# Layer 1 of a mixed network: the x weights of all nine taps made once per sample, and four engine queues in a planned order

## The chip, the cores and the metric

The kernel runs on one core of a Trainium2 chip, in one launch. Its time is the device time of that core in microseconds. It computes a network of four layers on eight images; the change touches the second one, layer 1, a deformable convolution.

## What is computed

Each image has 256 channels and 32x32 pixels. Layer 1, cut to what matters:

```python
def deform_conv(x, offset, w):     # x [B,64,32,32], offset [B,18,32,32]: (dy,dx) per tap of 3x3
    ...
    py = gy + ky + dy              # where each tap of each pixel looks
    px = gx + kx + dx
    ...
    sampled = corner(y0, x0, wy0 * wx0) + corner(y0, x0 + 1, wy0 * wx1) \
            + corner(y0 + 1, x0, wy1 * wx0) + corner(y0 + 1, x0 + 1, wy1 * wx1)
    return einsum('bckhw,ock->bohw', sampled, w)
xd = relu(group_norm(conv1x1(x, w1), g1, b1))     # 256 -> 64 channels
offset1 = conv3x3(xd, w_off)                      # 64 -> 18
out = deform_conv(xd, offset1, w_def) + xd
out = relu(group_norm(conv1x1(out, w3), g3, b3)) + x
```

A bilinear sample is a sum over all pixels of the image, each weighted by a hat function of its distance in y times one in x: the weight is -min(|d| - 1, 0) in each direction, and zero for all but four pixels. The kernel uses this form.

## The kernel before

`fast1` is layer 1. Its generators are cut into steps by `yield`, and the order in which the steps are written into the program is set by `by_time`: each stream has a start, a distance between its steps and a generator, and the stream that is due first goes next. One unit of that time is one tap; a sample takes nine. The compiler then schedules each engine's queue from that order and from what depends on what.

`before(b)` loads a sample's `x` (L1769), takes it to 64 channels (`c1`, L1774; the two halves of the image lie in partitions 0 to 63 and 64 to 127 of `xd`), normalizes it, and computes the 18 offsets (`off`, L1799). `pos` (L1808, L1809) holds for every tap the y and x positions of the 1024 pixels. `pos` is stored to DRAM as `shifts` (L1811, four stores).

`taps(b)` multiplies `xd` by each tap's 64x64 weights, 128 pixels at a time, into `z` (L1825, L1835); every second result is copied out of PSUM by VectorE, every other one by ScalarE (L1828, L1838).

`main` runs over 8 samples x 9 taps. For each tap the row of x positions and the row of y positions are read from `shifts` and spread over 128 partitions (`row`, L1885, 512 KB each, two ahead). A partition stands for one source pixel of a group of 128 (four image rows); eight groups are handled as columns. ScalarE makes the distances in x (`ax`, L1896) and in y (`ay`, L1902, and for the image rows beyond a group's own L1906 to L1912); VectorE subtracts 1 and cuts at 0 (L1914, L1915), and multiplies the two into `wt` (L1917, L1921). Two taps later `add` (L1866) lets TensorE accumulate `z` times `wt` into `acc`, which holds the sample's whole image in PSUM. The accumulation of a sample begins at L1850, with the skip connection.

`after(b)` takes the finished sum `s` (copied at L1873) back to 256 channels (`c3`, L1937, copied out at L1938), normalizes (`group_norm`, L1747 to L1764), adds `x`, loaded again as `xr` (L1932), and stores the result (L1944, L1945).

Layers overlap. `net.head()` runs the next layer's first steps, up to its `HOLD`, between the last steps of the layer before; for layer 1 these are its weights and `before(0)`. What lies behind `HOLD` needs SBUF and PSUM space that the layer before gives back. `in_order` ties the instructions of an engine to the order in which they were traced; before the change, layer 0 alone uses it.

Of the kernel before, what the change touches and what calls it, by code (L numbers as in the profile page):

```python
# [18 lines left out]
B = 8  # L19
# [878 lines left out]
class Fast:  # L898


    def __init__(self, ctx, tc, dram, out):
        self.tc, self.nc, self.dram, self.out = tc, tc.nc, dram, out
        nc = self.nc
        self.const = ctx.enter_context(tc.tile_pool(name="const", bufs=1))
        self.dpool = ctx.enter_context(tc.tile_pool(name="acts", bufs=1, space=bass.MemoryType.DRAM))
        self.ident = self.const.tile([P, P], F32, name="ident")
        make_identity(nc, self.ident)
        self.unit = self.const.tile([P, P], F32, name="unit")
        nc.gpsimd.memset(self.unit, 1.0)
        self.mean = self.const.tile([P, P], F32, name="mean")  # L910
        nc.gpsimd.memset(self.mean, 1.0 / C)
        self.mean64 = self.const.tile([P, 64], F32, name="mean64")
        nc.gpsimd.memset(self.mean64, 1.0 / C)
        self.eps5 = self.constant(1e-5, "eps5")
        self.eps6 = self.constant(1e-6, "eps6")
        self.sums2 = self.dpool.tile([2 * B, HF], F32, name="sums2")
        self.sums3 = self.dpool.tile([8 * B, N], F32, name="sums3")
        self.shifts = [self.dpool.tile([2, 9, N], F32, tag=f"shifts{b}", name=f"shifts{b}") for b in range(B)]
        self.sums = self.dpool.tile([8 * B, HF], F32, name="sums0")
        self.groups, self.following, self.lent = {}, None, {}  # L920
# [236 lines left out]
def fast0(net, io):  # L1157
# [8 lines left out]
    with ExitStack() as ctx, ExitStack() as att:  # L1166
# [528 lines left out]
        by_time(rest + [[T * B + 9, 0.3, gates(B - 1, BY_PRODUCTS)], [T * B + 4, 1, net.head()]])  # L1695
# [3 lines left out]
def fast1(net, io):  # L1699
    tc, nc = net.tc, net.nc  # L1700
    D = 64
    with ExitStack() as ctx:
# [29 lines left out]
        axs = [wp.tile([P, R], F32, tag=f"ax{i}", name=f"ax{i}") for i in range(2)]  # L1732
        ays = [wp.tile([P, R + HF], F32, tag=f"ay{i}", name=f"ay{i}") for i in range(2)]
        for a in axs + ays:
            nc.gpsimd.memset(a, 0.0)
        xds, zs, ss, own = ({} for _ in range(4))
        pools, stored = [psM], set()

        def group_norm(x, gsel, g, b):


            n, halves = x.shape[1], x.shape[2] // HF
            st = two.tile([P, n, halves, 6], F32, tag=f"gn_st{n}", name="gn_st")
            mv = two.tile([P, 2, n], F32, tag=f"gn_mv{n}", name="gn_mv")
            for k in range(n):
                for h in range(halves):
                    nc.vector.bn_stats(st[:, k, h, :], x[:, k, bass.ts(h, HF)])  # L1747
                nc.vector.bn_aggr(mv[:, :, k], st[:, k])
            yield
            pm = bank("gn_m")  # L1750
            nc.tensor.matmul(pm[:, :n], lhsT=gsel, rhs=mv[:, 0], start=True, stop=True)
            t = two.tile([P, 4, n], F32, tag=f"gn_t{n}", name="gn_t")
            mean, d, var, shift = (t[:, i] for i in range(4))
            nc.vector.tensor_copy(mean, pm[:, :n])
            nc.vector.tensor_tensor(d, mv[:, 0], mean, ALU.subtract)
            nc.vector.tensor_tensor(var, d, d, ALU.mult)
            nc.vector.tensor_tensor(var, var, mv[:, 1], ALU.add)
            yield
            pv = bank("gn_v")
            nc.tensor.matmul(pv[:, :n], lhsT=gsel, rhs=var, start=True, stop=True)  # L1760
            net.rsqrt(d, pv[:, :n], net.eps5)
            nc.vector.tensor_tensor(d, d, g, ALU.mult)
            nc.vector.tensor_tensor(shift, mean, d, ALU.mult)
            nc.vector.tensor_tensor(shift, b, shift, ALU.subtract)  # L1764
            yield d, shift

        def before(b):
            x = one.tile([P, KC, N], F32, tag="x", name="x")
# [3 lines left out]
            for k in range(KC):  # L1772
                for h in range(2):
# [3 lines left out]
                    )  # L1777
            xd = xds[b] = two.tile([P, HF], F32, tag="xd", name="xd")
            nc.scalar.copy(xd, ps)
            yield  # L1780
            for norm in group_norm(xd.unsqueeze(1), gsel1, col(G1), col(B1)):
                yield
            nc.scalar.activation(xd, xd, AF.Relu, scale=norm[0], bias=norm[1])
            xp = xpads[b % 2]
            nc.vector.tensor_copy(xp[:, 1:17, 1 : 1 + IMG], img(xd))
            nc.scalar.copy(xp[0:64, 17, 1 : 1 + IMG], xd[64:128, 0:IMG])
            nc.scalar.copy(xp[64:128, 0, 1 : 1 + IMG], xd[0:64, HF - IMG : HF])
            yield

            pos = two.tile([P, HF], F32, tag="pos", name="pos")  # L1790
            pss = [bank("off") for _ in range(2)]
            for t in range(5):
# [11 lines left out]
                if t % 2:  # L1804
                    yield
            for h in range(2):
# [3 lines left out]
                for xy in range(2):  # L1810
                    nc.sync.dma_start(  # L1811
                        out=net.shifts[b][xy, :, bass.ts(h, HF)], in_=pos[64 * h + 9 * xy : 64 * h + 9 * xy + 9]
                    )
            stored.add(b)
            yield

        def taps(b):
# [3 lines left out]
            for c in range(4):  # L1821
                for h, copy in enumerate((nc.vector.tensor_copy, nc.scalar.copy)):
# [5 lines left out]
                    copy(z[:, 4 * h + c, :8].rearrange("p t o -> p (t o)"), ps)  # L1828
                    yield

            for h, copy in enumerate((nc.vector.tensor_copy, nc.scalar.copy)):
# [6 lines left out]
                copy(z[:, 4 * h : 4 * h + 4, 8], ps[:, : 4 * D].rearrange("p (c o) -> p c o", o=D))  # L1838
                yield

        def main():

            wts, accs = {}, {}
# [11 lines left out]
            def add(b, t):  # L1855
# [15 lines left out]
                if t == 8:  # L1871
                    ss[b] = own["r"].tile([P, N], F32, tag="s", name="s")
                    nc.scalar.copy(ss[b], acc)  # L1873
# [5 lines left out]
            def load(i, xy):  # L1879

                if i < len(steps):
                    b, t = steps[i]
                    assert b in stored
                    rows[i, xy] = row = own["rows"].tile([P, N], F32, tag=f"row{xy}", name=f"row{xy}")
                    nc.sync.dma_start(out=row, in_=net.shifts[b][xy, t : t + 1, :].to_broadcast([P, N]))  # L1885

            for i in range(2):
                for xy in range(2):
                    load(i, xy)
            for i, (b, t) in enumerate(steps):  # L1890
                ky = t // 3 - 1

                ax, ay = axs[t % 2], ays[t % 2]
                mine = slice((1 + ky) * IMG, (1 + ky) * IMG + N)
                px = rows.pop((i, 0))
                nc.scalar.activation(ax[:, mine], px, AF.Abs, bias=col(NQX))  # L1896
                load(i + 2, 0)
                if i > 1:
                    add(*steps[i - 2])
                yield  # L1900
                py = rows.pop((i, 1))
                nc.scalar.activation(ay[:, mine], py, AF.Abs, bias=col(NQR))  # L1902
                far = ay[:, R:].rearrange("p (c n) -> p c n", c=8)
# [5 lines left out]
                else:  # L1909
# [3 lines left out]
                load(i + 2, 1)  # L1913
                nc.vector.tensor_scalar(ax, ax, -1.0, 0.0, ALU.add, ALU.min)  # L1914
                nc.vector.tensor_scalar(ay, ay, -1.0, 0.0, ALU.add, ALU.min)  # L1915
                wt = wts[b, t] = own["wt"].tile([P, 8, 6 * IMG], F32, tag="wt", name="wt")
                nc.vector.tensor_tensor(  # L1917
                    wt[:, :, : 4 * IMG], ay[:, :N].rearrange("p (c n) -> p c n", c=8),
                    ax[:, :N].rearrange("p (c n) -> p c n", c=8), ALU.mult,
                )  # L1920
                nc.vector.tensor_tensor(  # L1921
                    wt[:, :, 4 * IMG :], far, ax[:, 4 * IMG :].rearrange("p (c n) -> p c n", c=8)[:, :, :64], ALU.mult
                )
                yield
            for s in steps[-2:]:
                add(*s)
                yield

        def after(b):
            s = ss[b]  # L1930
            x = own["r"].tile([P, KC, N], F32, tag="xr", name="xr")
            nc.sync.dma_start(out=x, in_=io.src[b])  # L1932
            c3 = own["r"].tile([P, KC, N], F32, tag="c3", name="c3")
            for k in range(KC):
                for h in range(2):
                    ps = bank("c3")
                    nc.tensor.matmul(ps, lhsT=w3[:, bass.ts(k, P)], rhs=s[:, bass.ts(h, HF)], start=True, stop=True)  # L1937
                    nc.scalar.copy(c3[:, k, bass.ts(h, HF)], ps)  # L1938
                yield
            for norm in group_norm(c3, gsel3, vec[:, G3 : G3 + KC], vec[:, B3 : B3 + KC]):  # L1940
                yield
            for k in range(KC):
                nc.scalar.activation(c3[:, k], c3[:, k], AF.Relu, scale=norm[0][:, k : k + 1], bias=norm[1][:, k : k + 1])
                nc.vector.tensor_tensor(x[:, k, :], x[:, k, :], c3[:, k], ALU.add)  # L1944
            nc.sync.dma_start(out=io.dst[b], in_=x)  # L1945
# [7 lines left out]
        own["rows"] = io.pool(ctx, "f1p", 2)  # L1953
        pools.append(io.pool(ctx, "f1n", 2, PSUM))
# [4 lines left out]
        taps_of_all = main()  # L1959
        streams = [(0, 0.5, taps_of_all)]  # L1960
        for b in range(B):
            if b:
                streams.append((T * (b - 1) + 0.7, 0.6, before(b)))
            streams.append((T * b - 3.1 if b else -1, 0.32 if b else 0.05, taps(b)))
            streams.append((T * (b + 1) + 2.3, 0.6, after(b)))
        rest = by_time(streams, until=taps_of_all)
# [1510 lines left out]
```

## Time and profile before

| | |
|---|---|
| median of 14 runs | 3995.0 us (3986.57 to 4004.31) |
| the profiled execution | 3989.45 us, span 3987.6 us |
| busy, whole span | PE 92%, DVE 63%, ACT 57%, POOL 17% |
| granted clock of TensorE, whole span | 0.958 |
| layer 1's first and last accumulating matmul (L1866) start | 1260.2 and 1632.9 us |

PE is TensorE, DVE VectorE, ACT ScalarE, POOL GpSimd, SP SyncE, which issues most DMAs; PEld are PE's weight loads. A line of a group of instructions has the source line, engine, operation, what is written and read with its shape, the count, then busy microseconds, mean nanoseconds of one, and the engine's idle time just before, with what ended it. A line of the windows view has a stretch, its length, each engine's busy time in it (with the number of instructions), the granted clock, the mean busy share of the 16 DMA engines and GB/s. A line of the waits view says who waited for whom: total microseconds, times, longest. Matmuls are pipelined and their ends are modelled; many matmuls of the same tile run side by side in the array, so the mean of one is longer than its share of the time.

### The profile page before, as it was taken

To read this page: it belongs to the slowest core of one execution; us is meant where nothing else is said; L and a number is where in the kernel's file an instruction comes from. 1 tells how busy PE (TensorE), PEld (TensorE's weight loads), DVE (VectorE), ACT (ScalarE), POOL (GpSimd) and SP (SyncE) were. 2 spreads that over 40 slices of the span, in tenths; PEclk is the share of its full clock that TensorE was granted. 3 is DMA by queue.
4 is the path that set the end of the run, shared out by engine and by line. 5 is a ranking of instruction groups with operands and counts; after the bars stand their busy time and mean duration, and the time that the engine had idled before them with its cause. 6 is when DMAs were issued, how large, how long until landed. Compare 5 with 4: busy or idle time off the path is not lost. (4 is left out here: it accounts for less than half of the span.)

```text
span 3987.6 us, 70125 instructions
## 1 busy us (share of the span) xinstructions
PE 3678.5 (92%) x28022; PEld 1699.3 (43%) x28022; DVE 2516.0 (63%) x5026; ACT 2290.7 (57%) x3106; POOL 689.4 (17%) x850
## 2 busy tenths in 40 slices
PE   8999999999899887899999869989999999998997
PEld 3223333333234444444444436553333333327886
DVE  2489999999987988522322457732555656567355
ACT  4566666666545777434343455417677667774453
POOL 1101111101010000000000024330000240054653
PEclk9999999999998988899999979989999999999998
DMA  3314323323234877301000123332320130155676
GB/s 118 90 56 124 116 97 104 115 93 94 72 102 152 285 270 256 125 1 41 23 22 22 43 77 115 113 122 71 112 92 33 59 103 33 36 173 182 211 234 208
DMA packets 191506, 438.11 MB, mean 110 GB/s; under 512 B 22201, under 2 KB 117388, under 8 KB 178628
## 3 DMA queue, kind: packets, MB, share of 16 engines
q1 hardware_dynamic: 149188, 317.34, 24.4%
q0 software_dynamic: 38320, 111.08, 8.8%
q8 instruction: 224, 3.67, 0.4%
q10 hardware_dynamic: 3664, 5.11, 0.4%
q14 instruction: 110, 0.90, 0.1%
HBM read 280.20 MB, written 160.18 MB: 110 GB/s over the span
## 5 line engine op out<-in xcount | busy, mean ns | idle before, releaser
L2876 ACT ACTIVATE e<-s,five 128x1024 f32<-128x1024 f32 x512 | 542.3, 1111 | 216.1 <-PE s L2870 204.0
L1291 DVE SCALAR_TENSOR_TENSOR a<-hp,w_f_vec,a 128x961 f32<-128x961 f32 (+1 forms) x496 | 608.3, 1233 | 26.9 <-ACT a L1534 17.1
L2870 PE MATMUL s<-q,k 32*128 32x512 f32 x2048 | 312.7, 641 | 1.4 <-issue 0.9
L2850 PE MATMUL A<-e,v 128*32 128x512 f32 x2048 | 274.7, 608 | 17.0 <-DVE o L2855 15.2
L1465 ACT ACTIVATE e<-s 128x1024 f32<-128x1024 f32 x256 | 247.3, 1017 | 30.7 <-PE s L1459 27.3
L2558 DVE SCALAR_TENSOR_TENSOR junk<-mo_x,w_f_wr 128x256 f32<-128x256 f32 x512 | 250.1, 489 | 13.5
L1403 PE MATMUL A<-e,va 128*32 128x512 f32 x2048 | 249.3, 605 | 0.0
L1026 PE MATMUL pi<-xn,w_l_wpi 128*32 128x512 f32 x2048 | 238.0, 603 | 11.0 <-DVE xn L1281 8.9
L1420 DVE TENSOR_TENSOR sum<-sum,e 128x1024 f32<-128x1024 f32 x188 | 221.0, 1219 | 29.0 <-ACT e L1465 29.0
L1866 PE MATMUL acc<-wt,z 128*64 128x192 f32 (+4 forms) x1344 | 132.8, 338 | 51.7 <-DVE wt L1921 51.4
L1058 POOL DMA_INDIRECT res<-y,to x149 | 149.5, 1004 | 129.3 <-DVE y L3101 65.0
L3077 PE MATMUL h<-xk,w 128*128 128x128 f32 x1192 | 153.4, 282 | 20.1 <-DVE xk L3063 14.4
L2870 PEld LDWEIGHTS s<-q,k 32*128 32x128 f32 x2048 | 92.9, 183 | 169.5 <-issue 163.4
L3046 ACT COPY w<-w_l3f_w 128x512 f32 x149 | 91.6, 628 | 124.7 <-PE h L3077 84.8
L1459 PE MATMUL s<-q,k 32*128 32x512 f32 x1024 | 156.2, 647 | 6.7 <-ACT e L1465 6.7
L3077 PEld LDWEIGHTS h<-xk,w 128*128 128x128 f32 x1192 | 149.6, 197 | 26.6 <-DVE xk L3063 15.8
L1058 POOL DMA_INDIRECT so<-xl,rows x128 | 130.0, 1016 | 171.2 <-issue 126.8
L3097 PE MATMUL y<-w_l3f_w,hid 128*128 x596 | 146.6, 388 | 4.7 <-issue 2.7
L1866 PEld LDWEIGHTS acc<-wt,z 128*64 128x64 f32 x1344 | 99.0, 152 | 101.4 <-DVE wt L1921 72.8
L1026 PEld LDWEIGHTS pi<-xn,w_l_wpi 128*32 128x32 f32 x2048 | 67.4, 111 | 163.9 <-issue 133.6
L1531 ACT ACTIVATE hp<-pi,pib 128x512 f32<-128x512 f32 x128 | 85.9, 686 | 89.3 <-PE pi L1026 87.2
L2184 POOL TENSOR_TENSOR x<-x,yn 128x1024 f32<-128x1024 f32 x16 | 37.3, 2351 | 572.5 <-ACT yn L2183 324.3
(425 smaller groups left out, 6985.5 us busy)
## 6 DMA issues: line engine op xcount, KB each, us to landing
row<-shifts SPq DMA_DIRECT2D x144, 512.0 KB
x<-d SPq DMA_DIRECT2D x31, 1024.0 KB
xs<-so SPq DMA_DIRECT2D x73, 260.0 KB
so<-zero SPq DMA_DIRECT2D x5, 3380.0 KB
thrice<-vimg POOLq DMA_DIRECT2D x64, 256.0 KB
xl<-mox SPq DMA_DIRECT2D x64, 256.0 KB
yg<-res SPq DMA_DIRECT2D x32, 512.0 KB
gated<-st POOLq DMA_DIRECT2D x28, 512.0 KB
```

The costliest lines, as they stand in the source:

```text
L1026: self.nc.tensor.matmul(ps[32 * h : 32 * h + 32], lhsT=lhsT[:, 32 * h : 32 * h + 32], rhs=rhs, **flags)
L1058: made = self.nc.gpsimd.indirect_dma_start(**args)
L1291: nc.vector.scalar_tensor_tensor(to, fr, taps(t_), to, ALU.mult, ALU.add)
L1403: nc.tensor.matmul(state["A"][32 * h : 32 * h + 32, c, :], lhsT=vas[b][:, kt, c, 32 * h : 32 * h + 32], rhs=e[h // 2][:, h % 2, :], start= ...
L1420: nc.vector.tensor_tensor(half, half, e[j], ALU.add)
L1465: nc.scalar.activation(es[i][j], ss[j], AF.Exp, scale=SCALE)
L1866: nc.tensor.matmul(acc[o, a * IMG : e * IMG], lhsT=zs[b][:, c, t, :], rhs=wt[:, c, (a - lo) * IMG : (e - lo) * IMG], start=False, stop=(t ...
L2558: nc.vector.scalar_tensor_tensor(junk, xn[:, t, :], 1.0, self.wr[:, e, :], ALU.mult, ALU.mult, accum_out=pr[:, t, e : e + 1])
L2850: nc.tensor.matmul(A[32 * h : 32 * h + 32], lhsT=vs[b][:, kt, c * P + 32 * h : c * P + 32 * h + 32], rhs=e[:, h, :], start=first, stop=last,)
L2870: nc.tensor.matmul(ss[h // 2][:, h % 2], lhsT=ks[b][32 * h : 32 * h + 32, c, bass.ts(kt, P)], rhs=qs[b][32 * h : 32 * h + 32, c, bass.ts(h ...
L2876: anchor[:] = [nc.scalar.activation(e[:, 2 * j : 2 * j + 2], ss[j], AF.Square, scale=SCALE, bias=five)]
L3077: nc.tensor.matmul(ps[:, j, m], lhsT=ws[j][:, k, bass.ts(m, P)], rhs=xk[:, j, k], start=(k == 0), stop=(k == KC - 1),)
```

## The change

The hat function in x depends on the image column of the source pixel and not on its image row: 32 partitions hold all that the 128 of a group need, for every group. So the change makes the x weights of all nine taps of a sample at once, in `before`: TensorE spreads each tap's row of positions over 32 partitions by a matmul with one column of the identity, for four quarters of the image side by side; ScalarE takes the distance out of PSUM, VectorE cuts it, and four DMAs store it in DRAM as `hats` (nine taps, 32 columns, 1024 pixels). For each tap `main` then loads finished x weights, spread from 32 to 128 partitions by the DMA, straight into `ax`. The x positions are no longer stored.

Beside that:
- all of `z` leaves PSUM by ScalarE, and its small last part by VectorE;
- VectorE's min over `ay` leaves out columns that aren't read;
- there are three `ax` and three `ay`; `hx` shares the buffer of `x`; the `x` of sample 1 lies where `c3` will be, in a pool opened behind `HOLD`;
- the stores of y positions, `hats` and results are issued by GpSimd;
- steps are cut finer, and a table (`BEFORE`, `TAPS`, `AFTER`) gives each one its place in units of taps; from time 0 on, the queues of TensorE, VectorE, ScalarE and SyncE keep the order of the table;
- the half of `before(1)` with negative times and all of `taps(0)` are traced ahead of that; in layer 0, `head` steps follow each other at 0.4 instead of 1, as there are more of them.

```diff
 before(b), behind the offsets:
-                for xy in range(2):
-                    nc.sync.dma_start(
-                        out=net.shifts[b][xy, :, bass.ts(h, HF)], in_=pos[64 * h + 9 * xy : 64 * h + 9 * xy + 9]
-                    )
+                nc.gpsimd.dma_start(
+                    out=net.shifts[b][1, :, bass.ts(h, HF)], in_=pos[64 * h + 9 : 64 * h + 18]
+                )
+                yield
             stored.add(b)
+
+            for n in range(6):
+                if n < 5:
+                    ps = bank("hx")
+                    for i in range(2 if n < 4 else 1):
+                        for j in range(4):
+                            r = 64 * (j // 2) + 2 * n + i
+                            nc.tensor.matmul(
+                                ps[32 * j : 32 * j + 32, bass.ts(i, C)],
+                                lhsT=net.ident[:, r : r + 1].to_broadcast([P, 32]), rhs=pos[:, bass.ts(j % 2, C)],
+                                start=True, stop=True,
+                            )
+                if n == 1:
+                    hx = one.tile([P, 9 * C], F32, tag="x", name="hx").rearrange("p (t n) -> p t n", n=C)
+                if n:
+                    part = slice(2 * n - 2, min(9, 2 * n))
+                    nc.scalar.activation(
+                        hx[:, part], held[:, : C * (part.stop - part.start)].rearrange("p (t n) -> p t n", n=C),
+                        AF.Abs, bias=col(NQX),
+                    )
+                held = ps
+                yield
+            nc.vector.tensor_scalar(hx, hx, -1.0, 0.0, ALU.add, ALU.min)
+            for j in range(4):
+                nc.gpsimd.dma_start(
+                    out=net.hats[b][:, :, bass.ts(j, C)].rearrange("t q n -> q t n"), in_=hx[32 * j : 32 * j + 32]
+                )
             yield
 main:
-                px = rows.pop((i, 0))
-                nc.scalar.activation(ax[:, mine], px, AF.Abs, bias=col(NQX))
...
+            def load(i):
+                if i < len(steps):
+                    b, t = steps[i]
+                    assert b in stored
+                    nc.sync.dma_start(
+                        out=axs[i % 3][:, place(t)], in_=net.hats[b][t].unsqueeze(0).to_broadcast([P // IMG, IMG, N])
+                    )
...
+            def weights(i):
+                b, t = steps[i]
+                ax, ay, mine = axs[i % 3], ays[i % 3], place(t)
+                far = ay[:, mine.stop : mine.stop + HF]
+                used = ay[:, mine.start : mine.stop + (448, 480, 512)[t // 3]]
+                nc.vector.tensor_scalar(used, used, -1.0, 0.0, ALU.add, ALU.min)
...
+            for i, (b, t) in enumerate(steps):
+                load(i + 2)
+                if i + 1 < len(steps):
+                    distances(i + 1)
+                    fetch(i + 3)
+                yield
+                if i > 1:
+                    add(*steps[i - 2])
+                yield
+                weights(i)
                 yield
 the order:
-        taps_of_all = main()
-        streams = [(0, 0.5, taps_of_all)]
-        for b in range(B):
-            if b:
-                streams.append((T * (b - 1) + 0.7, 0.6, before(b)))
-            streams.append((T * b - 3.1 if b else -1, 0.32 if b else 0.05, taps(b)))
-            streams.append((T * (b + 1) + 2.3, 0.6, after(b)))
-        rest = by_time(streams, until=taps_of_all)
+        BEFORE = (
+            -9, -6.7, -6.2, -5.5, -4.4, -3.8, -2.8, -2.3, -1.6, -1, -0.5, 1.1, 1.4, 1.7, 2, 2.3, 3, 3.2,
+            3.9, 4.2, 4.5, 4.8, 5.1, 5.4, 5.9,
+        )
+        TAPS = [1.6 + 0.72 * n + 0.5 * i for n in range(10) for i in range(2)]
+        AFTER = (
+            1.9, 1.95, 5.6, 6, 6.1, 6.5, 6.6, 7, 7.1, 7.5, 7.6, 7.8, 8.4, 9.3, 9.8, 10.6, 11, 11.6, 12.2, 12.5, 12.8, 13.4, 13.5
+        )
...
+        planned(0, [n + h for n in range(T * B + 2) for h in (0, 0.3, 0.7)], main_steps)
+        for b in range(B):
+            if b:
+                planned(T * (b - 1), BEFORE, before(b))
+            planned(T * (b - 1), TAPS, taps(b))
+            planned(T * (b + 1), AFTER, after(b))
+        times.sort(key=lambda t_: t_[0])
...
+        run(0)
+        kinds = mybir.EngineType
+        with net.in_order(kinds.PE, kinds.DVE, kinds.Activation, kinds.SP):
+            run(T * B + 2)
```

`fetch(i)` loads the row of y positions of a tap as `load(i, 1)` did, `distances(i)` is ScalarE's part of the old loop for y, and `weights(i)` ends with the two products of the old loop.

## The prediction

> **What bounds the kernel now.** I read the page first: the span is 3987.6 us and PE is busy for 92% of it, so I looked for the stretch in which the changed function works, by asking for layer 1's accumulating matmul (L1866): 1260 to 1633 us. Then I cut that stretch into sample periods. ACT copies the finished sum `s` once per sample (L1873), and the timeline of ACT gives the marks:
>
> ```profile
> 1304.60 0.99 ACT L1873 COPY s<-acc 128x1024 f32<-128x1024 f32 x1
> 1594.08 0.99 ACT L1873 COPY s<-acc 128x1024 f32<-128x1024 f32 x1
> 1633.25 1.01 ACT L1873 COPY s<-acc 128x1024 f32<-128x1024 f32 x1 [7.23 <-PE acc L1866]
> ```
>
> The columns are start and duration. Samples 0 to 6 are six periods apart: 289.48/6 = 48.25 us. The last period, with no next sample to prepare, took 39.2 us. The windows view says who is full in two such periods, and in a stretch of layer 0, whose queues already follow a plan:
>
> ```profile
> core 0: us, PE busy (x) PEld busy (x) DVE busy (x) ACT busy (x) POOL busy (x), PEclk, DMA share, GB/s
> 1351.50:1398.40 46.90, 39.33 (x267) 20.88 (x264) 42.33 (x70) 35.58 (x50) 0.00 (x0) 0.92 0.81 284
> 1398.40:1445.30 46.90, 41.50 (x258) 20.88 (x260) 42.35 (x69) 34.06 (x49) 0.00 (x0) 0.85 0.82 277
> 900.00:1000.00 100.00, 99.07 (x1092) 35.11 (x1088) 90.51 (x87) 60.29 (x77) 10.08 (x18) 1.00 0.32 101
> ```
>
> DVE is busy for 90% of a layer 1 period. PE is busy for some 85%, at a clock of 0.85 to 0.92, against 99% at 1.00 in layer 0. Over the six 46.9 us windows from 1304.6 to 1586.0 the means are PE 39.2, DVE 42.2, ACT 35.2, DMA 0.79, clock 0.90. Scaled to 48.25 us: PE 40.4 (idle 7.9), DVE 43.4, ACT 36.2, DMA 38.0. The waits between 1245 and 1630 name the releaser, DVE's weights, and show ACT waiting for rows:
>
> ```profile
> PEld acc L1866 <- DVE wt L1921: 72.1, 41, 3.9
> PE acc L1866 <- DVE wt L1921: 51.4, 31, 3.6
> ACT ay L1902 <- DMA row<-shifts: 18.8, 19, 2.0
> ```
>
> So DVE bounds the stage, and PE, idle in between, loses clock as well.
>
> **The change part by part.** The prices are rows of the groups by form, 1245 to 1630 us (mean ns after the busy time):
>
> ```profile
> L1917 DVE TENSOR_TENSOR wt<-ay,ax 128x1024 f32<-128x1024 f32 x72 | 87.6, 1216 | 0.5
> L1896 ACT ACTIVATE ax<-row,w_f_vec 128x1024 f32<-128x1024 f32 x71 | 81.1, 1142 | 20.4 <-DMA row<-shifts 8.9 <-DVE ay L1915 6.2 <-DVE wt L1921 5.2
> L1915 DVE TENSOR_SCALAR ay<-ay 128x1664 f32<-128x1664 f32 x72 | 73.5, 1020 | 5.2 <-ACT ay L1906 4.1 <-ACT ay L1912 0.9
> L1914 DVE TENSOR_SCALAR ax<-ax 128x1152 f32<-128x1152 f32 x72 | 54.2, 753 | 15.6 <-ACT ax L1896 15.4
> L1828 DVE COPY z<-z 128x512 f32<-128x512 f32 x32 | 21.7, 686 | 0.2
> L1828 ACT COPY z<-z 128x512 f32<-128x512 f32 x28 | 16.0, 582 | 18.7 <-PE z L1825 18.6
> ```
>
> *DVE, per sample.* Nine L1914 go: 6.8. L1914 and L1915 differ by 267 ns for 512 elements; `used` is 160 elements shorter than 1664 on average, 83 ns x 9: 0.75. Four z copies go to ACT: 2.7. One z8 copy (L1838, 0.42) comes, and one min over 2304 elements, by the same slope 1.35. DVE: 43.4 - 8.5 = 34.9.
>
> *ACT.* Nine L1896 go: 10.3. Four z copies come (2.3), a z8 copy goes (0.37). The packed Abs are four of 512 columns at 0.71 (L1908's row) and one of 256, about 0.5: 3.3. ACT: 31.1.
>
> *PE.* New are 36 matmuls of ident columns on `pos`, 128x256 into 32 columns each. The nearest row has this shape, four column groups side by side as here:
>
> ```profile
> 1230.31 15.43 PE L1026 MATMUL po<-w_l_wpo,st 128*32 128x256 f32 x256
> ```
>
> That is 60 ns an instruction, and a matmul is two (off: 252 rows for seven samples of 18). 72 x 60 ns = 4.3 us per sample, and PE has no cover for it. But PE's 40.4 us are at clock 0.90, and a lower clock is paid in full:
>
> ```profile
> 1419.17 5.29 PE L1799 MATMUL off<-xpad,w_f_woff 64*32 64x512 f32 x18
> 1424.70 2.76 PE L1799 MATMUL off<-xpad,w_f_woff 64*32 64x512 f32 x18
> ```
>
> The same 18 instructions take twice as long in one place as in the other. At full clock I get 40.4 x 0.90 = 36.2, plus 4.3: 40.5 us. At the old clock it is 44.7. I take 40.5, since a PE with short waits has clock 1.00 in layer 0's window above, and keep 44.7 for the range.
>
> [...]
>
> *DMA.* Per step one 512 KB broadcast of `ax` from `hats` takes the place of one of `row`: equal. New are the `hats` stores, 1152 packets of 1 KB per sample. In the trace's packet records 1 KB packets take 51 ns on average at 2300 to 2400 us and 69 at 3600 to 3700; over 16 engines 3.7 to 5.0 us, I take 4. DMA: 38 + 4 = 42. Part of the 38 is crowding: 4 KB packets average 195 ns here, 159 in the median, so the floor is nearer 36. That the broadcast now reads 32 different rows has no row here; I price it between the median and the mean of a packet, -36 to 0 ns for 1152 packets: -2.6 to 0 us, and take 0.
>
> *Queues.* The `shifts` and output stores leave SP, where row loads stood behind them (L1811 and L1945 held SP 28.6 and 17.5 us), for POOL, which was idle throughout these windows. POOL gets seven issues a sample, at 0.70 (L1499's row) some 5 us. SP now stops at `load(i + 2)` until DVE has done `weights(i - 1)`; behind it stand `fetch(i + 3)` and x loads, and both have two steps (some 9 us) before their readers. Once a sample `load` also waits for the `hats` stores: made at 5.9, asked for at 7, used at 9.7 steps, so 3.8 x 4.8 = 18 us for four issues, a write and a read. Hidden; if that cover were gone, each microsecond would delay `weights(0)`, eight times.
>
> [...]
>
> *In-order waits.* PE now stands at z's third matmul until DVE has freed an `off` bank (L1808 and L1809, 1.4 us), and at each norm matmul. Bounds: 0 if the plan's distances hold, 7.9 if PE keeps its idle time. I take 3, nearer the planned stage of layer 0 (1%) than the old queue, since three other engines are at 70 to 90% here.
>
> The new period is thus 40.5 + 3 = 43.5 (41 to 47): 6 x (48.25 - 43.5) = 28.5 us gained. The last period has DVE work of 30 us (9 x 2.84 and `after`'s 5 to 7), about 33 with waits: 6 gained.
>
> *The start.* `hx` of sample 0 falls into layer 0's tail, where PE is full (50.00 of 50 us from 1150 to 1200): +4. Sample 1's `x` was loaded at 1137, before layer 0 ended; now it lies in space that layer 0 still holds, and the first such load, `xr`, went out at 1256.6. From there: load 5, c1 3, norm and relu 8, off 4, and `add(0)`, behind `off` in PE's order, starts near 1276 instead of 1260. Less work remains to s(0) (eight steps of 4.3 rather than 44 us), so s(0) comes near 1310: +6. If the space is free from 1230 on, this is -8; if the chain crawls, +15.
>
> Sum: -28.5 - 6 + 4 + 6 = -24.5 on this execution's 3989.45 us (span 3987.6 and 1.85 around it). That execution lies 5.5 us below the median of 14 runs, 3995.0, so I say 3970.5.
>
> **The rivals.** *PE full, as in layer 0* (0.26): clock 1.00, half a microsecond idle, period 41, last period 31: -43.5 - 8 + 4 = -47.5, 3947. For it: layer 0's row. Against it: DMA would be at 90% or more.
>
> *PE's waits stay* (0.18, slower): a head that waits for ACT or DVE now holds everything behind it on PE, so the 7.9 us of idle time and the clock remain, and `hx` comes on top: 40.4 + 4.3 + 7.9 = 52.6. 6 x 4.35 + 10 at the start = +36, 4031. It decides once idle time and lost clock together exceed 48.25 - 40.5 = 7.8 us a period. For it: ACT now evicts every z (18.6 us of waits on z already) and `hx`. Against it: 72 waits of PE on `wt` made most of the idle time, and `wt` gets 8.5 us cheaper.
>
> *DMA takes over* (0.10, no change): if 4 KB packets crept from 195 to 235 ns, 2304 of them need 33.8, the 384 of 8 KB at 410 ns 9.9, `hats` 5: 48.6 us. 6 x 0.4 more, 6 gained in the last period and 10 lost at the start: +6, 4001.
>
> **How the numbers follow.** My forecast has 0.46; its own range is 3955 to 3988. This kernel can be told from no change by about 0.2%, 8 us. Faster: 0.44 of the forecast, all of PE full and 0.02 of DMA, 0.72. Same: 0.02 and 0.08, 0.10. Slower: 0.18. The range of 3938 to 4006 takes in PE full with 9 us to spare and the DMA case; the slower case lies mostly outside.
>
> **What would show it.** The distance of the L1873 copies falls to 41 to 47 us; DVE's share drops to about 80%, PE's passes 90% with the clock at 0.95 or above; PE's waits on `wt` shrink to a third. `hx` should cost near 4.3 us of PE. I am wrong if PE's idle time stays near 8 us, if DVE waits for `ax` from DMA, or if the first `add` comes later than 1280.

## The result, and the profile after: slower by 6.3%

The changed kernel takes 4247.4 us (median of 9 runs, 4234.0 to 4255.0) against 3994.7 us before (43 runs): a ratio of 1.0631 [1.0617, 1.0645], 253 us more. Its profiled execution took 4246.97 us, with a span of 4245.2 us. No case that I had priced went beyond 4031 us.

The page already says where. These are its slices of 106 us, in tenths:

```profile
PEclk9999999999997777769999997999999999999998
DMA  3323333331225555540001002433232032045666
```

Layer 1 lies in the slices with a clock of 7 and a DMA share of 5; before, DMA was at 0.79 there. The marks are again ACT's copies of `s` (start, duration):

```profile
1353.79 0.99 ACT L1990 COPY s<-acc 128x1024 f32<-128x1024 f32 x1
1835.80 0.99 ACT L1990 COPY s<-acc 128x1024 f32<-128x1024 f32 x1
1892.64 1.01 ACT L1990 COPY s<-acc 128x1024 f32<-128x1024 f32 x1 [6.50 <-PE acc L1905]
```

Six periods take 482.0 us, 80.3 each instead of 48.25; the last takes 56.8 instead of 39.2. The next layer's first matmul, `qk`, starts at 1913.8 instead of 1651.2. Of these 262.6 us, 192.5 come from the six periods (482.0 - 289.5), 49.2 from the start (first copy at 1353.8 instead of 1304.6), 17.7 from the last period and 3.2 from what follows. The span grew by 257.6, so what follows gave back only 5 us.

The windows view, with the columns as before: first the six periods, then three short stretches inside one of them.

```profile
core 0: us, PE busy (x) PEld busy (x) DVE busy (x) ACT busy (x) POOL busy (x), PEclk, DMA share, GB/s
1353.80:1835.80 482.00, 306.37 (x1973) 155.76 (x1975) 221.26 (x339) 181.54 (x287) 25.30 (x41) 0.74 0.56 174
1445.00:1449.50 4.50, 4.50 (x54) 2.36 (x52) 3.55 (x6) 2.93 (x5) 0.52 (x1) 1.00 0.27 102
1450.00:1452.00 2.00, 1.36 (x19) 0.99 (x16) 1.75 (x2) 1.81 (x3) 0.00 (x0) 1.00 0.99 274
1460.50:1466.00 5.50, 5.49 (x48) 2.54 (x40) 3.13 (x6) 2.48 (x4) 0.00 (x0) 0.89 0.27 99
```

No engine is full: DVE is busy for 221.3 of 482 us, ACT for 181.5, PE for 306.4 at a clock of 0.74. DMA as a mean is far from full too, at 0.56. But the short stretches show two kinds of time: all 16 DMA engines at 0.99 for some 2 us, then a plateau at 0.27, about 4 engines of 16, for some 5 us. In the trace's packet records the plateau moves about 23.5 packets of 4 KB per us at 0.17 us each: 4.0 engines are busy. What is it that runs there? SP's timeline:

```profile
1449.52 0.53 SPq L1923 DMA_DIRECT2D ax<-hats  x1
1456.72 0.31 SPq L1933 DMA_DIRECT2D row<-shifts  x1
1457.13 0.52 SPq L1923 DMA_DIRECT2D ax<-hats  x1
1465.77 0.32 SPq L1933 DMA_DIRECT2D row<-shifts  x1
```

Each `ax` load is followed by a pause of 7 to 9 us until the next `row` goes out. And the waits in the same 482 us (who waited for whom, total us, times, longest; SPq is SP's queue):

```profile
SPq L1933 <- DMA row<-shifts: 240.4, 49, 9.2
ACT ay L1939 <- DMA row<-shifts: 221.8, 46, 11.0
DVE wt L1961 <- DMA ax<-hats: 84.1, 28, 8.6
PEld acc L1905 <- DVE wt L1961: 22.5, 8, 6.2
```

DVE waits for `ax`, which the prediction named as a sign that it is wrong; ACT waits even more for `row`, whose own loads were not changed, only put into one queue with those of `ax`. SP itself stands for half of the time at the issue of a `row` until an earlier one has landed, 240.4 us against 20.0 in the six periods before: its pauses are late landings again. The engines' own work is what was predicted, with PE's stretched by the clock:

```profile
L1961 DVE TENSOR_TENSOR wt<-ay,ax 128x1024 f32<-128x1024 f32 x54 | 66.2, 1225 | 92.5 <-DMA ax<-hats 84.1 <-PE c L1995 6.8
L1939 ACT ACTIVATE ay<-row,w_f_vec 128x1024 f32<-128x1024 f32 x54 | 62.0, 1148 | 263.8 <-DMA row<-shifts 221.8 <-DVE wt L1961 39.7 <-DVE pos L1819 2.3
L1832 PE MATMUL hx<-pos,ident 128*32 128x256 f32 x432 | 37.9, 502 | 28.7 <-ACT z L1866 28.7
L1849 POOL DMA_DIRECT2D hats<-hx x24 | 15.3, 649 | 95.8 <-DVE hx L1847 95.8
```

The theory made from this (A): the one DMA that spreads `hats` has a source of the shape [4, 32, 1024], the four copies outermost, and is given to 4 DMA engines instead of 16. An estimate agrees roughly. Per tap, each of these four engines moves 128/4 = 32 packets of `ax` and, if `row` is spread evenly over 16, 128/16 = 8 of `row`; a 4 KB packet takes 0.2074 us on average here: 40 x 0.2074 x 9 taps = 74.7 us per sample. With sixteen 8 KB packets of `x` and `xr` at 0.47 us that is 82 us, and GpSimd's stores add some 6 us if they are spread evenly over 16. Measured: 80.3. The averages are too long for these four, as they take in the bursts: a 4 KB packet took 178 ns where it started among 7 or fewer, 226 among 15 or more.

The packet records say it without a sum. Over the six periods at least 4 packets are under way for 99% of the time, and exactly 4 for 45% of it; before, exactly 4 for 1% and fewer for 9%. So four engines are busy nearly all the time, and the mean over 16 hides it.

What the shape of a source does to the number of engines I had not weighed. For [4, 32, 1024] the plateau shows 4.0 of them; e4 and e8, below, test it.

### The profile page after: what moved, and what is told of

Its sections match the earlier page's. It is cut to its first block, busy times and chain, and to the rows that moved or that the text cites. A ratio compares the mean times of both kernels' runs of the same rounds, so it can differ in the third digit from the quotient of the medians.

```text
span 4245.2 us, 71321 instructions
## 1 busy us (share of the span) xinstructions
PE 3757.1 (89%) x28598; PEld 1733.0 (41%) x28598; DVE 2470.8 (58%) x4938; ACT 2258.8 (53%) x3101; POOL 727.1 (17%) x910
## 5 line engine op out<-in xcount | busy, mean ns | idle before, releaser
L2948 PE MATMUL A<-e,v 128*32 128x512 f32 x2048 | 274.5, 608 | 17.7 <-DVE o L2953 16.0
L1939 ACT ACTIVATE ay<-row,w_f_vec 128x1024 f32<-128x1024 f32 x72 | 82.7, 1149 | 334.9 <-DMA row<-shifts 280.2
L1027 PE MATMUL pi<-xn,w_l_wpi 128*32 128x512 f32 x2048 | 240.4, 606 | 17.7 <-DVE xn L1282 11.3
L1961 DVE TENSOR_TENSOR wt<-ay,ax 128x1024 f32<-128x1024 f32 (+1 forms) x144 | 131.8, 955 | 118.9 <-DMA ax<-hats 110.0
L1905 PE MATMUL acc<-wt,z 128*64 128x192 f32 (+4 forms) x1344 | 141.3, 366 | 45.9 <-DVE wt L1961 45.9
L3175 PEld LDWEIGHTS h<-xk,w 128*128 128x128 f32 x1192 | 149.5, 197 | 24.1 <-DVE xk L3161 13.3
L1905 PEld LDWEIGHTS acc<-wt,z 128*64 128x64 f32 x1344 | 110.7, 168 | 99.1 <-DVE wt L1961 64.9
```

The costliest lines, as they stand in the source:

```text
L1027: self.nc.tensor.matmul(ps[32 * h : 32 * h + 32], lhsT=lhsT[:, 32 * h : 32 * h + 32], rhs=rhs, **flags)
L1905: nc.tensor.matmul(acc[o, a * IMG : e * IMG], lhsT=zs[b][:, c, t, :], rhs=wt[:, c, (a - lo) * IMG : (e - lo) * IMG], start=False, stop=(t ...
L2948: nc.tensor.matmul(A[32 * h : 32 * h + 32], lhsT=vs[b][:, kt, c * P + 32 * h : c * P + 32 * h + 32], rhs=e[:, h, :], start=first, stop=last,)
L3175: nc.tensor.matmul(ps[:, j, m], lhsT=ws[j][:, k, bass.ts(m, P)], rhs=xk[:, j, k], start=(k == 0), stop=(k == KC - 1),)
```

## The experiments

The kernels were run in four groups, on three chips, so each is compared with the kernel before in its own group: 3935.3 us for the first four, 4010.6 for the next four, 4007.0 for e9 and e10, 3934.7 for e11. Periods are the mean of the six from the first to the seventh copy of `s`. The rivals of A were the planned order, now forced on four queues, and the price of the new packets (another source, a smaller destination).

**e1: the broadcast as four DMAs of 32 partitions** (everything else as after).

```diff
-                    nc.sync.dma_start(
-                        out=axs[i % 3][:, place(t)], in_=net.hats[b][t].unsqueeze(0).to_broadcast([P // IMG, IMG, N])
-                    )
+                    for c in range(P // IMG):
+                        nc.sync.dma_start(
+                            out=axs[i % 3][c * IMG : c * IMG + IMG, place(t)], in_=net.hats[b][t]
+                        )
```

> The changed kernel; only the load of the x weights differs: four DMAs of 32 partitions each instead of one whose source is [4, 32, 1024]. Theory A (the one broadcast runs on 4 of the 16 DMA engines, and they carry the stage): the distance of the s copies falls from 80 us to what the other terms of the prediction allow, 41 to 47 us, and the time to 3950 to 3985 us. Theory B (the planned order stalls: SP's head waits for the load's buffer and holds the rows behind it): period and time stay, 4150 us or more.

Measured: 3979.3 us, 1.0118 [1.0098, 1.0138]. The window of its six periods:

```profile
1316.50:1638.30 321.80, 255.28 (x2010) 130.16 (x2010) 220.44 (x339) 176.67 (x285) 25.24 (x41) 0.89 0.91 253
```

The period falls from 80.3 to 53.6 us: moving the same bytes by DMAs that are not led by a 4 takes back most of the loss. The size was missed, since I had expected the predicted period. DMA is now the bound at 0.91, and for another reason: a 4 KB packet takes 253 ns on average, against 195 before. Each of the new DMAs writes to 32 partitions only, and there are four where there was one; the runs do not separate the two, and why these packets take longer was not shown. With one DMA over 128 partitions a packet takes 184 ns in e5, below. Packets can be this slow in another way too: e8, below, has 265 ns with every DMA over 128 partitions.

**e2: after, without the forced order; e3: e1, without it.** Both leave out the same line:

```diff
-        with net.in_order(kinds.PE, kinds.DVE, kinds.Activation, kinds.SP):
-            run(T * B + 2)
+        run(T * B + 2)
```

> The changed kernel without the forced order of the four queues; the one broadcast of the x weights is kept. Theory A: still 4 engines, so the period stays at 65 us or more and the time at 4130 us or more. Theory B: the period falls under 50 us and the time to 4010 us or less.

> Both edits: four DMAs of 32 partitions for the x weights, and no forced order. Against e1 this prices the planned order alone. Theory A with an order that removes PE's idle time: 10 to 25 us slower than e1, near 3985 us. If the order does nothing: within 8 us of e1. Theory B: this one is the fastest of all and e1 is slow.

```profile
1324.90:1794.10 469.20, 321.02 (x1998) 164.35 (x1997) 217.23 (x338) 182.01 (x287) 25.02 (x41) 0.77 0.54 176
```

That is e2: 4161.1 us in one run, +226, period 78.2. With every queue free to be scheduled by the compiler, DMA share (0.54), clock (0.77) and period stay near after's 0.56, 0.74 and 80.3: the order is not the cause of the loss. At most some 27 of the 253 us go with it, about what it costs in e5 against e6, below. e3 took 3991.6 us, 1.0146 [1.0124, 1.0168], with a period of 55.1; 12 us above e1, which is the direction expected of an order that helps; but the intervals overlap, so the order did at most little there, in either direction.

**e4: the kernel before, with its x rows spread from a [4, 32, 1024] source.** The reverse test: one old broadcast takes the new shape, and nothing else of the change is there. It reads the same row and writes the same tile.

```diff
-                    nc.sync.dma_start(out=row, in_=net.shifts[b][xy, t : t + 1, :].to_broadcast([P, N]))
+                    src = net.shifts[b][xy, t : t + 1, :]
+                    src = src.unsqueeze(0).to_broadcast([4, P // 4, N]) if xy == 0 else src.to_broadcast([P, N])
+                    nc.sync.dma_start(out=row, in_=src)
```

> The kernel before; only the source of the x rows' broadcast is written as [4, 32, 1024] instead of [128, 1024], the same bytes into the same tile. Theory A: the load takes over 5 us at a quarter of the DMA engines; a tap costs those four engines 32 + 8 packets of 4 KB at 0.165 to 0.20 us, 6.6 to 8.0 us, so the period is 62 to 80 us instead of 48 and the time 4100 to 4250 us. Theory B: no change, 3980 to 4005 us.

```profile
1335.10:1823.50 488.40, 290.39 (x1576) 152.87 (x1576) 262.50 (x420) 216.65 (x304) 0.00 (x0) 0.70 0.54 159
```

```profile
ACT ax L1898 <- DMA row<-shifts: 148.4, 27, 16.2
DVE ax L1916 <- ACT ax L1898: 108.3, 24, 14.3
```

4184.5 us in one run: +249 against 3935.3, after's whole loss, from the shape of one source. Period 81.4, DMA share 0.54, clock 0.70. Exactly 4 packets are under way for 46% of these six periods, fewer for 4%. The sum for four engines, with 24 packets of 8 KB a sample at 0.44 us, gives 40 x 0.2184 x 9 + 10.5 = 89 us, a tenth too much as in after. Theory A is shown with no other part of the change present.

**e8: the same with eight copies outermost** (`[8, 16, 1024]`; the diff is e4's with 8 for 4).

> The kernel before; the x rows' source written as [8, 16, 1024]. If the first dimension of the source sets the number of DMA engines: eight engines, 16 + 8 packets a tap, 4.0 to 4.8 us of each tap's 5.4, so between e4 and before: 10 to 80 us above before, against some 250 us in e4.

```profile
1314.80:1708.20 393.40, 261.20 (x1576) 135.04 (x1576) 261.61 (x420) 216.65 (x303) 0.00 (x0) 0.80 0.76 199
```

4137.0 us in one run, +126; period 65.6. It lies between before and e4, as expected of eight engines, but costs more than I had expected, because packets became dearer, 265 ns: 24 packets of 4 KB a tap on eight engines are 24 x 0.265 x 9 = 57.2 us, and 24 of 8 KB add about 10. Exactly 8 packets are under way for 31% of the time, fewer for under 4%: here eight engines are the full ones. Why they take so long here no run shows.

**e5: the copies innermost, so that one DMA covers 128 partitions and no 4 leads its source.** The pixels of a group are taken image column first: partition p holds column p // 4 of row p % 4. Then the source is [32, 4, 1024]. The distances in y get other constants, and `z` needs its left operand in that order, which costs one strided copy by ScalarE per sample (`xq`); for its space `pos` has a single buffer.

```diff
-    in_=net.hats[b][t].unsqueeze(0).to_broadcast([P // IMG, IMG, N])
+    in_=net.hats[b][t].unsqueeze(1).to_broadcast([IMG, P // IMG, N])
...
-    -col(p // IMG), 4 - col(p // IMG)
+    -col(p % 4), 4 - col(p % 4)
...
+            xq = xqs[b] = one.tile([P, HF], F32, tag="xq", name="xq")
+            nc.scalar.copy(xq.rearrange("p (c x y) -> p c x y", c=4, y=4), xd.rearrange("p (c y x) -> p c x y", c=4, y=4))
```

> The changed kernel with the 128 source pixels of a group in another order, image column first: the x weights then come by one DMA over all 128 partitions whose source is [32, 4, 1024]. To pay for it, z's left operand is a copy of xd in that order (one ScalarE copy a sample) and pos has one buffer. [...] Theory B2 (reading 32 different rows, or the total DMA load, is what costs): packets stay near 250 ns, period 52 to 55, 1.01 of before.

```profile
1318.60:1600.40 281.80, 251.16 (x2008) 129.88 (x2006) 219.23 (x340) 186.27 (x292) 25.31 (x41) 0.94 0.83 300
```

4006.7 us, 0.9996 [0.9986, 1.0007]: no change against before, with everything else of the change in place. That is not the 1.01 of theory B2, nor the gain that I expected if writing 32 partitions at a time is what costs: 0.98 to 0.995, from packets of 160 to 200 ns, a DMA share of 0.80 to 0.88 and a period of 42 to 47 us. All of these came but the time: a 4 KB packet takes 184 ns (median 159), the DMA share is 0.83, 13.3 of 16 engines on average, and the period is 47.0 us, with PE busy for 89% of it at a clock of 0.94. `hx` comes out at its price:

```profile
L1834 PE MATMUL hx<-pos,ident 128*32 128x256 f32 x432 | 27.5, 384 | 2.9 <-ACT z L1868 2.3 <-DVE pos L1821 0.6
```

27.5/6 = 4.6 us per sample, predicted 4.3; the same line takes 6.3 in after (37.9/6), at the lower clock.

**e6: e5 without the forced order** (e2's diff).

> e5 without the forced order of the four queues: what the order is worth once the DMA is out of the way. If the order removes PE's idle time: e6 is 10 to 30 us slower than e5. If it does nothing: within 8 us. If the order itself costs: e6 is faster than e5.

```profile
1313.70:1584.90 271.20, 249.79 (x1999) 129.77 (x1998) 213.67 (x339) 186.56 (x291) 25.45 (x41) 0.98 0.87 306
```

3985.4 us, 0.993 [0.9915, 0.9945]: faster than before and after, 25 us below before. The period is 45.2 us and PE is busy for 92% of it at a clock of 0.98. The forced order, which cost nothing that could be told in e3, costs 21 us here. Part of that is at the start: the first accumulation comes 35 us after layer 0's last `po` matmul in e5, 21 us in e6 (15 before).

**e9, e10, e11: whose order costs it.** e9 is e5 with SP left out of the forced order, e10 is e5 with SP alone in it, and e11 is e5 with the order of two steps in a tap exchanged, so that SP asks for a row before it stands at a load of `ax`:

```diff
e9   -        with net.in_order(kinds.PE, kinds.DVE, kinds.Activation, kinds.SP):
     +        with net.in_order(kinds.PE, kinds.DVE, kinds.Activation):
e10  +        with net.in_order(kinds.SP):
e11  in the steps of a tap: load(i + 2) behind fetch(i + 3) instead of ahead of it
```

> e5 with the order kept for TensorE, VectorE and ScalarE, and SyncE's queue left free. Theory C (SP's head costs: it waited 57.6 us for hats stores and 50 us for weights in e5, with row loads behind it, and ScalarE waited 49 us for rows): as e6, 0.990 to 0.995 of before, the period near 45 us. Theory D (the order of the computing engines costs, by a late first accumulation and norm chains in front of ready work): as e5, 0.998 to 1.002.

> e5 with only SyncE's queue in the planned order. Theory C: as e5, 0.998 to 1.002 of before. Theory D: as e6, 0.990 to 0.995, with the first accumulation 20 us behind layer 0's last po matmul as in e6 (35 in e5).

> e5 with the planned order on all four queues; in each tap SyncE's fetch of the next y row now stands before the load of the x weights instead of behind it. If the load's waits for hats stores and weights (57.6 and 50.1 us over six samples in e5) hold back the rows that ScalarE waits for (49.1 us): that wait falls under 20 us, the period from 47.0 to 44 to 46, and the time to 0.992 to 0.997 of before. If the rows are late for another reason: 0.998 to 1.002, the wait as before.

e9: 4049.5 us, 1.0098 [1.0082, 1.0114]. e10: 4020.4 us, 1.0023 [1.0009, 1.0038]. e11: 3936.5 us, 1.0005 [0.9995, 1.0016]. None came out as a theory of one guilty queue wants it: with order on three engines and none on SP the period grows to 53.5, with SP alone it is 50.3, both above e5 (all four) and e6 (none). The late start does follow one part of the order, that of the computing engines: the first accumulation comes 33 us after layer 0's last `po` matmul in e9, 21 in e10. In e11 the wait that I had suspected is almost gone, from e5's

```profile
ACT ay L1941 <- DMA row<-shifts: 49.1, 18, 4.8
```

```profile
SPq L1925 <- DMA hats<-hx: 57.6, 12, 11.3
```

to e11's

```profile
ACT ay L1941 <- DMA row<-shifts: 45.8, 13, 9.5
```

```profile
SPq L1925 <- DMA hats<-hx: 9.8, 4, 4.6
```

(all from 1316 to 1590 us), and neither ACT's wait for rows nor the time moved. SP now stands longer elsewhere (at `row` until an earlier one has landed: 54 us instead of 20). So the stop at `hats` did not set the time by itself. What the order costs beyond the 14 us at the start stays open; it isn't the cost of one queue alone, and it depends on how the four match.

**e7: the kernel before, with each x row as four DMAs of 32 partitions**, to price such DMAs away from the change.

```diff
-                    nc.sync.dma_start(out=row, in_=net.shifts[b][xy, t : t + 1, :].to_broadcast([P, N]))
+                    for c in range(0, P, 128 if xy else 32):
+                        n = 128 if xy else 32
+                        nc.sync.dma_start(out=row[c : c + n], in_=net.shifts[b][xy, t : t + 1, :].to_broadcast([n, N]))
```

> The kernel before; only each x row's broadcast is split into four DMAs of 32 partitions, all of the same source row. [...] Theory B2: packets stay near 195 ns and the time within 10 us of before.

```profile
1304.70:1679.20 374.50, 285.37 (x1584) 156.41 (x1584) 270.90 (x420) 214.39 (x300) 0.00 (x0) 0.72 0.71 203
```

4106.0 us, 1.0226 [1.0207, 1.0246]. The packets take 241 ns against 195, not what theory B2 wants; if writing 32 partitions at a time is what costs, I expected 230 to 260 ns and 25 to 60 us more. The time is over these bounds, at +95 us, with a DMA share of only 0.71 and a period of 62.4. So DMA's rate alone isn't what sets this kernel's period; SP waits for ACT's `ax` for 164 us here, against 88 before, so its row loads go out late. Why it does, no run shows. The run supports slower packets for 32 partitions and settles nothing more.

The main runs side by side:

| kernel | how x weights or x rows are spread | ratio, or us over before | period, us | 4 KB packet, ns | DMA share | clock |
|---|---|---|---|---|---|---|
| before | one row to 128 | | 48.25 | 195 | 0.79 | 0.90 |
| after | [4, 32, 1024] | 1.0631 | 80.3 | 207 | 0.56 | 0.74 |
| e4 | before, [4, 32, 1024] | +249 | 81.4 | 218 | 0.54 | 0.70 |
| e8 | before, [8, 16, 1024] | +126 | 65.6 | 265 | 0.76 | 0.80 |
| e1 | after, four DMAs of 32 | 1.0118 | 53.6 | 253 | 0.91 | 0.89 |
| e5 | after, [32, 4, 1024] | 0.9996 | 47.0 | 184 | 0.83 | 0.94 |
| e6 | e5, no forced order | 0.993 | 45.2 | 191 | 0.87 | 0.98 |

## Why the prediction was wrong

**The step that failed is the DMA term.** "Per step one 512 KB broadcast of `ax` from `hats` takes the place of one of `row`: equal." The bytes and the packets are equal; the engines that carry them are not. The four that carried `ax` were busy for nearly all of the 80.3 us of a period, where the sum said 42 for all 16. The next sentence asked the wrong question about the same DMA: "That the broadcast now reads 32 different rows has no row here", priced at -2.6 to 0 us. That price was sound: in e5, with the engines back (a DMA share of 0.83), a packet took 184 ns, between the two ends. But the shape of the source was not priced at all, and it was plain in the diff: `unsqueeze(0).to_broadcast([P // IMG, IMG, N])` puts 4 outermost, where the broadcast before had 128 partitions. The third rival, DMA takes over, went wrong in the same way: it let packets creep up on 16 evenly loaded engines, and could therefore not get beyond 4001.

The second signal of being wrong, a first `add` later than 1280, came as well (1298.3), and here the step was wrong for two reasons. Sample 1's load went out at 1246.3, earlier than the 1256.6 that I had built on, yet the norm chain behind it crawled: `off` waited until 1290.2, 12.4 us of it for `xpad`. In e5 the first `add` comes at 1279.5 and in e6 at 1271, against 1276 predicted; s(0) at 1318.6 and 1313.7 against 1310 (layer 0 ended at 1249.5 in after, 1244.1 in e5 and 1250.3 in e6). So most of the lateness went with the few-engine broadcast, which shares its queue with these loads, and the term "+6" was some 9 us short in e5; without the order, in e6, it was near.

**What held, once the broadcast had its engines:**
- *DVE* 34.9 us per sample: 36.5 in e5, 35.6 in e6. *ACT* 31.1: 31.0 and 31.1, with 1.1 for `xq`, which was not in the sum.
- *PE* 40.5 at full clock: 41.6 in e6 at 0.98. PE gave back its lost clock as the prediction hoped, and PE became the fullest engine. In after the same work took 51.1 us per sample, at 0.74: here the stalled stage paid a second time through the clock. The two `off` rows of the prediction, 5.29 and 2.76 us, agree: before's granted clock was 0.52 in the one stretch and 1.00 in the other.
- *DMA* 42: 39.0 in e5 and 39.3 in e6 (share times period). The 4 us for the `hats` stores came right by luck: they were priced as 1152 packets of 1 KB, and after's records have 256 of 4 KB at 214 ns and 64 of 2 KB at 117 ns a sample, 3.9 us over 16 engines.
- *GpSimd*: 24 issues of `hats` took 0.65 us each in after, priced at 0.70.

**What was undersized even so.** With its engines back the broadcast still doesn't bring the forecast: e5 is level with before, not 24.5 us below. Six periods of 47.0 instead of 43.5 are 21 us, and the first sum is 9 us late, as above; the last period, 32.4 us, came as forecast (33), and the 4 us in layer 0's tail don't show (its last `po` matmul starts at 1244.1, before at 1245.4, on another chip). The in-order waits were put at 3 us in a period of 43.5. e5 has 47.0 - 41.9 = 5.1 us of idle PE, e6, without the order, 45.2 - 41.6 = 3.6. e6's 25 us gained equal the predicted 24.5, but with another make-up: its six periods give less (45.2 rather than 43.5) and its last period, 38.8 us, gives nothing like the 6 us; so the equal number is luck. The cover of 18 us for `hats` was judged by distance in steps and called hidden: SP did wait there, 57.6/6 = 9.6 us a sample in e5, and in e11, where that wait shrank to 9.8 us in all, the time was the same.

**The slower rival** had the sign and not the mechanism. It kept PE's idle time at 7.9 us, for heads that wait for ACT or DVE; PE was idle for (482.0 - 306.4)/6 = 29 us, and behind it stood a transfer. The order that this rival was about is worth 21 us between e5 and e6, a twelfth of the loss.

## What to carry to other kernels

When a DMA changes its shape, price the engines that it runs on before its bytes: look at the outermost dimension (of the source, in these runs: 4 and 8 gave 4 and 8 engines), and divide the packets by the engines that this gives, added to what the same engines carry for others. In a profile, a DMA share that stands still near 4/16 (0.27 here) while everyone waits for DMA can be a full queue on a few engines, as it was here, and not an idle one; cut the windows shorter than one transfer to see it. If copies must be spread, put them innermost ([32, 4, N] and not [4, 32, N]), even when a reordering copy has to be paid for it: here that was 47.0 us a period against 80.3, and four DMAs of 32 partitions each were only a part of the way (53.6).

## What the runs showed of the hardware that was not expected

- The shape of a broadcast source alone, with the same bytes and packets, moved this kernel by 249 us (4 outermost) and 126 us (8 outermost).
- Where half of the spread rows were written to 32 partitions at a time, all 4 KB packets of the queue took 241 and 253 ns on average (e7, e1); where every DMA covered 128, 184 to 195 (e5, e6, before). With half of them led by a 4 it was 207 and 218 (after, e4), by an 8 265 (e8). The cause is open.
- A broadcast that reads 32 different rows, four times each, was no dearer per packet than one that reads a single row 128 times: 184 against 195 ns, 159 in the median of both.
- In e5's kernel a forced queue order was best whole or not at all: on four engines 0.9996 of before, on none 0.993, on three 1.0098, on SP alone 1.0023.
